# The first two row tiles of x in two transfers instead of one

## The chip, the cores and the metric

The kernel runs on one core of a Trainium2 chip. The metric is device time in microseconds (us): the median of three runs of the kernel before is 456.29 us (456.26 to 456.68).

## The reference

A graph network of three edge convolutions on N = 2500 nodes with 256 features and 80000 edges, sorted by target. Cut to what matters:

```python
h = maximum(layernorm(x), 0)                        # by row of x
xs = [h]
for W, b in ((W0, b0), (W1, b1), (W2, b2)):
    m = concat([h[dst], h[src] - h[dst]]) @ W + b   # one row for each edge
    s = segment_sum(m, dst, N)
    h = relu(s / maximum(count_of_edges, 1)[:, None])
    xs.append(h)
out = x + concat(xs) @ Wf + bf
```

## The kernel before, in words

Since a sum over edges is linear, the kernel builds the matrix of counts A (how often node m is a source of node n) and computes each layer as a product of A with h @ W_bottom, plus h @ (W_top - W_bottom). The 2500 rows of x lie in 20 tiles of 128 rows (the last has 68); the tile `acc` holds x by row tile (`acc[:, t, :]`), and later the running output.

The beginning, about the first 32 us, does three things side by side, in an order written out by hand as a string of short names, one for each step; each engine takes its own instructions strictly in that order:

- It prepares the search for the edges: `dst_i`, the list of targets, is loaded (line 434, on ACT's queue). VectorE casts its first column into `first`, a product on TensorE shifts it, VectorE makes masks (`after`, `behind`, `pick`), and at the end `start_i` holds where each block of edges begins. GpSimd then gathers the edges (`ed`, `es`) with it. Two copies of the edge lists in DRAM, `src_e` and `dst_e`, lengthened at the end, serve the last gather.
- It normalizes x, two row tiles at a time: `stats` (lines 746 to 754) takes mean and variance on VectorE (`st`, `mv`), ACT and VectorE make scale and offset (`rs`, `off`), and VectorE, ACT or GpSimd normalizes the tile in place. TensorE transposes it into `hT` and multiplies it with the weights (`own_w`).
- It builds A window by window: VectorE compares node numbers (`one_m`, `one_n`), and TensorE multiplies these masks.

The string of steps begins (st0 is the statistic of tiles 0 and 1, st1 of 2 and 3, st2 of 4 and 5, st4 of 8 and 9, st7 of 14 and 15):

```
dstr lim first st0 sq0 next pi0 pk00 sc0 pk01 pi1 sg00 of0 Nm0 T0 st1 se00 sg01 pk10 st2 se02 R0 sq1 sc1
of1 sg10 se01 se03 pk21 sg21 Z0 Np1 pk31 sg31 st4 T1 st7 ...
```

Loads of x go through `load_x` (line 438) by the list `chunks` (line 443): tiles 0 and 1, and 2 to 5, on SP's queue, tiles 6 to 11 on ACT's queue, then on SP's queue, between the weights, tiles 12 to 15 and 16 to 19 (the last, of 68 rows, by a transfer of its own). A transfer counts up one of eight completion semaphores, which the tile framework hands out in turn; a transfer that reuses one waits, on the issuing engine, until the one before it on that semaphore has landed, and what stands behind it on the engine waits too.

After the beginning, TensorE runs through the three layers and the final product.

Of the kernel before, what the change touches and what calls it, by code (L numbers as in the profile page):

```python
# [298 lines left out]
def by_windows(ctx: ExitStack, tc: tile.TileContext, x, src, dst, Ws, bs, Wf, bf, out, missing):  # L299
    nc = tc.nc  # L300
    PE, DVE, ACT, POOL, SP = nc.tensor, nc.vector, nc.scalar, nc.gpsimd, nc.sync
    PEo, DVEo, POOLo, ACTo, SPo = (InOrder(tc, e) for e in (PE, DVE, POOL, ACT, SP))
# [3 lines left out]
    NT = (N + P - 1) // P  # L306
# [131 lines left out]
    def load_x(queue, a, b):  # L438
        queue.dma_start(acc[:, a:min(b, NT - 1), :], xr[:, a:min(b, NT - 1), :])
        if b == NT:  # L440
            queue.dma_start(acc[:LAST, NT - 1, :], x[(NT - 1) * P:N, :])

    chunks = [(0, 2), (2, 6), (6, 12), (12, 16), (16, NT)]
    load_x(SPo, *chunks[0])
    load_x(SPo, *chunks[1])
    load_x(ACTo, *chunks[2])
    ws = [None] * L
    wfs = [None] * (L + 1)
    raws = [None] * (L + 1)
# [6 lines left out]
    def load_wb(l, queue=SP):  # L456
        if l:
            new_raw(l)
        ws[l] = wpool.tile([P, DC, D], F32, name="wt"), raws[l][:, :, 0, :] if l else hot.tile([P, DC, D], F32, name="own_w0", bufs=1)
        queue.dma_start(ws[l][1], Ws[l][D:2 * D, :].rearrange("(c p) d -> p c d", p=P))  # L460

    def load_wt(l, queue=SP):
        queue.dma_start(ws[l][0], Ws[l][0:D, :].rearrange("(c p) d -> p c d", p=P))

    def load_wf(l, queue=SP):
        if l == L:
            new_raw(l)
        wfs[l] = raws[l][:, :, 1, :] if l else hot.tile([P, DC, D], F32, name="own_w1", bufs=1)
        queue.dma_start(wfs[l], Wf[l * D:(l + 1) * D, :].rearrange("(c p) d -> p c d", p=P))

    load_wb(0, SPo)
    load_x(SPo, *chunks[3])
    load_wf(0, SPo)
    load_x(SPo, *chunks[4])
    load_wt(0, SPo)

    line_i = pp.tile([P, 1], I32, name="line_i")
# [1111 lines left out]
def gnn_kernel(tc: tile.TileContext, x, src, dst, Ws, bs, Wf, bf, out):  # L1589
    nc = tc.nc  # L1590
    with tc.tile_pool(name="flag", bufs=1) as flag:
        missing = flag.tile([1, 1], I32, name="missing")
        tc.mark_branch_hint_location("again", "LikelyTaken",
                                     engines=[getattr(mybir.EngineType, e) for e in ("PE", "DVE", "Activation")])
        near_end = by_windows(tc, x, src, dst, Ws, bs, Wf, bf, out, missing)
        loads, (again,) = nc.values_load_multi_w_load_instructions(missing, min_val=0, max_val=1)

        for d in loads:
            if d.ins.engine in [getattr(mybir.EngineType, e) for e in ("PE", "DVE", "Activation")]:
                tc.add_manual_dep(d.ins, near_end.ins.name,  # L1600
                                  mybir.DependencyInfo(mybir.DependencyClass.Sync, mybir.DependencyReason.DATA),
                                  reason="behind the outputs")
        with tc.If(again > 0, label="again"):
            general(tc, x, src, dst, Ws, bs, Wf, bf, out)
# [28 lines left out]
```

## Time and profile before

| | |
|---|---|
| median of three runs | 456.29 us |
| the profiled execution's own time | 456.32 us |
| its span, from first to last instruction | 454.4 us |
| mean granted TensorE clock | 0.998 |
| TensorE busy | 447.2 us, 98% of the span |
| VectorE busy | 379.3 us, 83% |
| ScalarE (ACT) busy | 327.7 us, 72% |
| GpSimd (POOL) busy | 52.0 us, 11% |

Busy shares are averages over the whole span; the change lies in its first 12 us, so the tables by stage and the timeline of that stretch say more. All times of the trace are counted from the span's start. Nearly every instruction carries line 267, a helper that records it in program order, so groups are told apart by the names of their tiles. A line of the timeline gives start, length, engine, line, instruction, output<-input, shapes, and in brackets how long the engine had been idle before it and what ended that. For an issue of a transfer (SPq, ACTq) the length is that of the issue on its engine, not that of the data.

### The profile page before, as it was taken

What the parts mean: (1) busy time and instruction counts of PE and PEld (TensorE: products, weight loads), DVE (VectorE), ACT (ScalarE), POOL (GpSimd) and SP (SyncE); (2) the same over time, 40 slices, a digit from 0 to 9 for tenths busy, and PEclk for the clock granted to TensorE, in tenths of its full rate; (3) what the DMA queues carried; (4) which work ended last, traced back from release to release, by engine and by line L of the source; (5) the groups of instructions that cost most, each with busy time, mean ns of one, the idle gap of its engine ahead of it and who ended that gap; (6) DMA issues with size and microseconds to landing.
All of it is one profiled execution on the core that took longest, in us unless ns stands there. A gap on an engine that the chain in (4) does not pass through costs nothing.

```text
span 454.4 us, 7514 instructions
## 1 busy us (share of the span) xinstructions
PE 447.2 (98%) x2749; PEld 360.6 (79%) x2749; DVE 379.3 (83%) x736; ACT 327.7 (72%) x608; POOL 52.0 (11%) x68
## 2 busy tenths in 40 slices
PE   8999999999999999999999999999999999999996
PEld 4878877888888888878877878877888778788795
DVE  7999999998899645399958968996999589598996
ACT  5898888777764445587879968875877899597730
POOL 4781201302015010100000000000000000000000
PEclk9999999999999999999999999999999999999999
DMA  8410198792949995611393442211114924322015
GB/s 277 117 36 1 33 202 154 86 160 45 207 93 122 189 244 123 145 47 45 103 359 124 137 169 93 91 45 47 46 53 135 337 92 147 127 92 91 1 52 178
DMA packets 28776, 55.05 MB, mean 121 GB/s; under 512 B 1995, under 2 KB 20126, under 8 KB 28734
## 3 DMA queue, kind: packets, MB, share of 16 engines
q0 software_dynamic: 12576, 19.06, 25.4%
q1 hardware_dynamic: 14654, 33.83, 22.2%
q10 hardware_dynamic: 1504, 1.63, 1.1%
q8 instruction: 22, 0.36, 0.3%
q14 instruction: 20, 0.16, 0.1%
HBM read 36.47 MB, written 18.20 MB: 120 GB/s over the span
## 4 chain that ended last, share of the span: by engine, by line
PE 92%; POOL 2%; DMA 2%; DVE 2%; issue 1%; ACTq 0%; POOLq 0%
PE bank L267 92%; DMA acc<-in_x_dram 2%; POOL acc L267 1%; DVE st L267 1%; POOL es L267 1%; POOL ed L267 0%; DVE acc L267 0%; DVE mv L267 0%; ACTq L267 0%; DVE end_f L267 0%; DVE start_i L267 0%; DVE rs L267 0%; DVE ends L267 0%; DVE off L267 0%; DVE lead L267 0%
## 5 line engine op out<-in xcount | busy, mean ns | idle before, releaser
L267 ACT CAST block<-staged 128x1008 fp32r<-128x1008 bf16 x120 | 117.6, 1029 | 3.5 <-ACT block L267 3.1
L267 PE MATMUL bank<-a,zh 128*128 128x504 f32 (+1 forms) x200 | 80.3, 401 | 0.0
L267 PE MATMUL bank<-block,zh 128*128 128x504 f32 (+1 forms) x200 | 79.0, 395 | 0.0
L267 PE MATMUL bank<-a,zl 128*128 128x504 f32 (+1 forms) x200 | 77.9, 389 | 0.0
L267 PE MATMUL bank<-block,zl 128*128 128x504 f32 (+1 forms) x200 | 77.2, 386 | 0.0
L267 ACT CAST a<-bank 128x480 fp32r<-128x480 f32 (+1 forms) x105 | 53.2, 570 | 26.5 <-PE bank L267 26.4
L267 DVE TENSOR_TENSOR one_m<-iota_m,key_m 128x2048 bf16<-128x2048 bf16 (+2 forms) x55 | 64.3, 1168 | 6.2 <-PE bank L267 5.8
L267 PE MATMUL bank<-block,sh 128*128 128x504 f32 x160 | 69.1, 432 | 0.0
L267 PE MATMUL bank<-block,sl 128*128 128x504 f32 x160 | 62.5, 391 | 0.0
L267 PE MATMUL bank<-block,staged 128*128 128x512 f32 (+1 forms) x288 | 62.4, 368 | 0.0
L267 PEld LDWEIGHTS bank<-block,staged 128*128 128x128 f32 x288 | 49.4, 188 | 9.9 <-issue 0.4
L267 DVE TENSOR_TENSOR block<-staged 128x1008 fp32r<-128x1008 bf16 x40 | 46.7, 1204 | 4.2 <-PE bank L267 3.4
L267 PEld LDWEIGHTS bank<-block,zh 128*128 128x128 f32 x200 | 37.6, 188 | 8.6 <-issue 0.4
L267 PEld LDWEIGHTS bank<-block,zl 128*128 128x128 f32 x200 | 37.5, 188 | 8.2 <-issue 0.4
L267 PEld LDWEIGHTS bank<-a,zl 128*128 128x128 f32 x200 | 37.7, 188 | 7.4 <-issue 0.5
L267 PEld LDWEIGHTS bank<-a,zh 128*128 128x128 f32 x200 | 37.6, 188 | 7.4 <-issue 0.5
L267 DVE TENSOR_TENSOR one_n<-iota_n,key_n 128x640 bf16<-128x640 bf16 (+2 forms) x110 | 42.5, 428 | 0.0
L267 PEld LDWEIGHTS bank<-block,sh 128*128 128x128 f32 x160 | 30.1, 188 | 10.6 <-issue 2.8
L267 PEld LDWEIGHTS bank<-block,sl 128*128 128x128 f32 x160 | 30.1, 188 | 9.4 <-issue 3.7
L267 PEld LDWEIGHTS <-one_m 128*128 128x128 bf16 x834 | 29.2, 98 | 7.4 <-issue 3.7
L267 PE MATMUL bank<-own_w,hT 128*128 128x256 f32 x144 | 34.6, 384 | 0.0
L267 PE MATMUL bank<-one_n,one_m 128*128 128x60 bf16 x834 | 32.5, 195 | 0.0
(198 smaller groups left out, 667.3 us busy)
## 6 DMA issues: line engine op xcount, KB each, us to landing
staged<-a_dram SPq DMA_DIRECT2D x52, 504.0 KB
a_dram<-a POOLq DMA_DIRECT2D x24, 630.0 KB, 9.3
acc<-in_x_dram POOLq DMA_DIRECT2D x3, 640.0 KB, 20.7
out_dram<-acc SPq DMA_DIRECT2D x5, 256.0 KB
acc<-in_x_dram SPq DMA_DIRECT2D x2, 512.0 KB
acc<-in_x_dram ACTq DMA_DIRECT2D x1, 768.0 KB
out_dram<-acc SPq DMA_DIRECT2D x5, 128.0 KB
wt<-in_L_gnn_W_dram SPq DMA_DIRECT2D x2, 256.0 KB
```

The lines of the kernel that those rows point to most:

```text
L267: return self.tc.keep_in_program_order(call(*args, **kwargs))
```

## The change

The entry (0, 2) of `chunks` becomes (0, 1) and (1, 2), and SP issues both. The entries behind it keep their tiles, queues and order.

```diff
-    chunks = [(0, 2), (2, 6), (6, 12), (12, 16), (16, NT)]
+    chunks = [(0, 1), (1, 2), (2, 6), (6, 12), (12, 16), (16, NT)]
     load_x(SPo, *chunks[0])
     load_x(SPo, *chunks[1])
-    load_x(ACTo, *chunks[2])
+    load_x(SPo, *chunks[2])
+    load_x(ACTo, *chunks[3])
...
     load_wb(0, SPo)
-    load_x(SPo, *chunks[3])
+    load_x(SPo, *chunks[4])
     load_wf(0, SPo)
-    load_x(SPo, *chunks[4])
+    load_x(SPo, *chunks[5])
     load_wt(0, SPo)
```

The first instructions on SP's queue, before the change. DMAHW0 to DMAHW7 are the eight semaphores; 128x2x256 is two row tiles; `own_w` and `wt` are weights, `brow` the rows of the bias:

```order
L267 DMA acc<-in_x_dram 128x2x256
L267 DMA acc<-in_x_dram 128x4x256
L267 DMA own_w_131<-in_L_gnn_W_dram 128x2x256
L267 DMA acc<-in_x_dram 128x4x256
L267 DMA own_w_134<-in_L_gnn_Wf_dram 128x2x256
L267 DMA acc<-in_x_dram 128x3x256
L267 DMA acc<-in_x_dram 68x256 [waits DMAHW0_49,DVE_49]
L267 DMA wt<-in_L_gnn_W_dram 128x2x256 [waits DMAHW1_49]
L505 DMA src_e<-in_src_dram 16x1250 [waits DMAHW2_49]
L495 DMA brow<-in_L_gnn_b_dram 1x256 [waits DMAHW3_49,Pool_49]
L495 DMA brow<-in_L_gnn_b_dram 1x256 [waits DMAHW4_49]
L504 DMA es_161<-in_src_dram 1x128 [waits DMAHW5_49,Pool_49]
```

The same place after the change:

```order
L267 DMA acc<-in_x_dram 128x256 x2
L267 DMA acc<-in_x_dram 128x4x256
L267 DMA own_w_132<-in_L_gnn_W_dram 128x2x256
L267 DMA acc<-in_x_dram 128x4x256
L267 DMA own_w_135<-in_L_gnn_Wf_dram 128x2x256
L267 DMA acc<-in_x_dram 128x3x256 [waits DMAHW0_49]
L267 DMA acc<-in_x_dram 68x256 [waits DMAHW1_49,DVE_49]
L267 DMA wt<-in_L_gnn_W_dram 128x2x256 [waits DMAHW2_49]
L506 DMA src_e<-in_src_dram 16x1250 [waits DMAHW3_49]
L496 DMA brow<-in_L_gnn_b_dram 1x256 [waits DMAHW4_49,Pool_49]
L496 DMA brow<-in_L_gnn_b_dram 1x256 [waits DMAHW5_49]
L505 DMA es_162<-in_src_dram 1x128 [waits DMAHW6_49,Pool_49]
```

There is one more issue at the head, so every issue behind it comes one place later, and the semaphores are handed out one further on. The wait for DMAHW0, which is that of `dst_i`, moves from the last 68 rows of x to the transfer of tiles 16 to 18. In the kernel before, `src_e` waits for DMAHW2, the transfer of tiles 2 to 5; now it waits for DMAHW3, and which transfer that is follows from VectorE's rows. Two places there: the first statistics (the BN_STATS rows, each of one row tile), behind the memset of `first`, and further on the statistic of tile 2. The first place, before:

```order
L267 MEMSET first 1x1 [waits DVE_49]
L267 BN_STATS st<-acc 128x6 [waits DMAHW1_49]
L267 BN_STATS st<-acc 128x6
L267 BN_AGGR mv<-st 128x2 [waits DVE_49] x2
L267 TENSOR_TENSOR after<-bank_228,after 128x1 [waits PE_49]
```

and after:

```order
L267 MEMSET first 1x1 [waits DVE_49]
L267 BN_STATS st<-acc 128x6 [waits DMAHW1_49]
L267 BN_STATS st<-acc 128x6 [waits DMAHW2_49]
L267 BN_AGGR mv<-st 128x2 [waits DVE_49] x2
L267 TENSOR_TENSOR after<-bank_229,after 128x1 [waits PE_49]
```

Tile 1's statistic now has a wait of its own; the order of VectorE's instructions is the same. The second place, up to the statistic of tile 2, after the change:

```order
L267 RECIPROCAL rs<-rs 128x2 [waits Activation_49]
L267 TENSOR_SCALAR behind<-limr_i,after 128x384
L267 SCALAR_TENSOR_TENSOR pick<-limr_i,first,behind 128x384 [waits DVE_49]
L267 SCALAR_TENSOR_TENSOR off<-mv,rs 128x2
L267 TENSOR_SCALAR acc<-acc,mv,rs 128x256
L267 BN_STATS st<-acc 128x6 [waits DMAHW4_49]
```

The last row waited for DMAHW2 before. So tiles 2 to 5 now have DMAHW4, and DMAHW3 stays with ACT's transfer of tiles 6 to 11: `src_e` now waits for that one, and the first `brow` row for tiles 2 to 5, the other way round than before.

## The prediction

> **What bounds the kernel now.** I read the page's first part, then the chain of waits, then busy time by stage, and last the instructions of SP, ACT and DVE in the first 12 us, where the change acts. The page and the table by stage (stretch in us, its length, then busy us and instructions of PE, PEld, DVE, ACT, POOL, the clock, the share of the 16 DMA engines, GB/s):
>
> ```profile
> span 454.4 us, 7514 instructions
> ...
> PE 447.2 (98%) x2749; PEld 360.6 (79%) x2749; DVE 379.3 (83%) x736; ACT 327.7 (72%) x608; POOL 52.0 (11%) x68
> ...
> 4.47:10.28 5.81, 5.37 (x22) 2.76 (x22) 5.56 (x28) 4.31 (x14) 0.73 (x2) 1.00 1.06 345
> 10.28:17.63 7.35, 7.35 (x42) 6.65 (x41) 7.33 (x37) 6.18 (x21) 5.56 (x6) 1.00 0.59 178
> ...
> 32.17:450.06 417.89, 417.87 (x2566) 338.50 (x2566) 350.76 (x619) 302.32 (x539) 30.15 (x31) 1.00 0.49 119
> ```
>
> From 32.17 us on TensorE is busy 417.87 of 417.89 us at full clock: nothing there waits for a load of x. What the change can move is the moment at which that stretch begins, one for one. Which work sets it stands in the chain of waits (start, length, what):
>
> ```profile
> 1.24 9.04 DMA acc<-in_x_dram
> ...
> 10.30 0.75 DVE st L267 x2
> ...
> 21.50 0.95 POOL es L267
> ...
> 32.17 417.89 PE bank L267 x2566
> ```
>
> The chain goes back to the transfer that ACT issued at 1.24 (row tiles 6 to 11) and through the row statistics on VectorE. VectorE is the narrow place of this stage: 5.56 of 5.81 us and then 7.33 of 7.35 us busy. A stall of it there, or an earlier start, goes through to the end with little lost. So the question is narrow: does VectorE start earlier or stall?
>
> **Where the loads and VectorE stand.** First the issues of SP and ACT, then VectorE with one weight load of TensorE (start, length, engine, instruction, what it waited for):
>
> ```profile
> 0.73 0.46 SPq L267 DMA_DIRECT2D acc<-in_x_dram  x1
> 0.81 0.40 ACTq L267 DMA_DIRECT2D dst_i<-in_dst_dram  x1
> 1.24 0.49 ACTq L267 DMA_DIRECT2D acc<-in_x_dram  x1
> 1.25 0.46 SPq L267 DMA_DIRECT2D acc<-in_x_dram  x1
> 1.75 0.51 SPq L267 DMA_DIRECT2D own_w<-in_L_gnn_W_dram  x1
> ...
> 3.49 0.47 SPq L267 DMA_DIRECT2D acc<-in_x_dram  x1
> ...
> 7.25 0.62 SPq L505 DMA_DIRECT2D src_e<-in_src_dram  x1
> 10.35 0.54 SPq L495 DMA_DIRECT2D brow<-in_L_gnn_b_dram  x2
> 11.09 0.22 SPq L504 DMA_DIRECT2D es<-in_src_dram  x1
> ```
>
> ```profile
> 4.47 0.15 DVE L267 CAST first<-dst_i 128x1 f32<-128x1 int32 x1 [1.86 <-DMA dst_i<-in_dst_dram]
> 4.67 0.42 DVE L267 BATCH_NORM_STATS2 st<-acc 128x6 f32<-128x256 f32 x1
> 4.68 0.06 DVE L267 MEMSET first<- 1x1 f32 x1
> 4.85 0.51 PEld L267 LDWEIGHTS bank<-first,shift 128*128 128x128 f32 x2 [0.97 <-POOL back_b L513]
> 5.00 0.41 DVE L267 BATCH_NORM_STATS2 st<-acc 128x6 f32<-128x256 f32 x1
> 5.55 0.12 DVE L267 TENSOR_TENSOR after<-bank,after 128x1 f32<-128x1 f32 x1
> ...
> 7.74 0.75 DVE L267 BATCH_NORM_STATS2 st<-acc 128x6 f32<-128x256 f32 x2
> ...
> 10.30 0.75 DVE L267 BATCH_NORM_STATS2 st<-acc 128x6 f32<-128x256 f32 x2
> 11.19 0.72 DVE L267 BATCH_NORM_STATS2 st<-acc 128x6 f32<-128x256 f32 x2
> ...
> 17.98 0.30 DVE L267 TENSOR_SCALAR lo_i<-es 128x256 int32<-128x256 int32 x1
> ```
>
> The first statistic of x at 4.67 stands behind two instructions on `dst_i`, which VectorE had awaited for 1.86 us: the cast at 4.47 that ends at 4.62, and a memset that needs the cast. So the 256 KB of tiles 0 and 1 were not what VectorE was held by for any time that shows: at most the 0.05 us from 4.62 to 4.67.
>
> **The change, part by part.** It takes out one issue of 256 KB and puts in two of 128 KB; the bytes and their order on SP's queue stay.
>
> 1. *Tile 0 comes earlier.* Its cover is `dst_i`. Even with tile 0 there at 3 us, the statistic cannot pass the cast and memset ahead of it. Gain: between 0 and 0.05 us (4.67 - 4.62), and the next step, 5.55, waits for a product on TensorE whose weight load began at 4.85 behind the memset, so not even that need come through. I take 0. If `dst_i` were not in the way, the cover would be gone and the gain would be tile 0's lead, which the next rows bound.
>
> 2. *`dst_i` itself could land earlier*, if tile 1's half leaves the DMA engines to it for a while. The packets of 0 to 2 us, then the rows of 3 to 4 us, and last of 4 to 4.5 us (q1 is SP's, q10 ACT's; packets, MB, share of the engines):
>
> ```profile
> DMA packets 18, 0.02 MB, mean 9 GB/s; under 512 B 0, under 2 KB 18, under 8 KB 18
> ...
> DMA packets 278, 0.38 MB, mean 382 GB/s; under 512 B 28, under 2 KB 193, under 8 KB 278
> q10 hardware_dynamic: 100, 0.21, 55.6%
> q1 hardware_dynamic: 178, 0.17, 49.9%
> ...
> q1 hardware_dynamic: 175, 0.18, 102.2%
> q10 hardware_dynamic: 1, 0.00, 0.1%
> ```
>
> Both queues share the engines while `dst_i` flows. At most tile 1's whole 128 KB would step aside: 131 KB / 382 GB/s = 0.34 us. But tile 1 is issued at about 0.73 + 0.52 = 1.25 us, where now the third tile is, well before tile 0's half can be through (the first row: 18 packets by 2 us), so the queue holds work all along. I take 0; bound 0.34 us of gain.
>
> 3. *One more issue on SP.* Price 0.46 us of the queue for 256 KB and 0.22 us for the smallest (es), 0.52 us from start to start at most. It pushes back, up to the load of `wt`, everything behind it: the 512 KB of tiles 2 to 5 from 1.25 to 1.75, the weights, tiles 12 to 15, and so on. Hidden by the queue's own backlog: in 4 to 4.5 us SP's queue alone fills the engines (102.2%) with what had been issued by 1.71. A transfer that is handed over 0.5 us later behind such a backlog lands no later. Bound if the backlog did not cover it: 0.52 us on a VectorE stall. The nearest place is the statistic at 7.74 of tiles 2 and 3; SP's wait below shows their transfer landed at about 7.25, so even there 0.5 us of slack stands against 0.52. The statistic at 11.19 reads tiles 12 and on; no row shows when those land, so there the bound stands in full. I take 0, the row being nearest to a queue that is never empty; bound 0.5.
>
> 4. *Waits that move.* Eight completion semaphores go round, and every issue waits for the one that used its semaphore before. SP's waits (total, times, longest):
>
> ```profile
> SPq L495 <- DMA acc<-in_x_dram: 2.4, 1, 2.4
> SPq L505 <- DMA acc<-in_x_dram: 1.3, 1, 1.3
> ```
>
> The instruction order shows the load of tiles 16 to 18 now behind `dst_i`, so it goes out at 4.47 and not 3.49: 1 us late. Its data are last in a backlog that keeps the engines over 100% (table: 1.06 up to 10.28), so the late hand-over is free. The copy of `src` into `src_e` changed its partner: it waited 1.3 us for tiles 2 to 5 and went out at 7.25; now it waits for ACT's 768 KB, which landed at 10.28. That is 3 us later, and behind it on SP stand the two `brow` rows (10.35 to about 11.0) and the `es` row (11.09 to about 11.6). `src_e` is read by the gather at 21.50 (the chain's POOL es), `es` by VectorE at 17.98: slack of 6 us and more. Cost 0; the bound without that slack would be 0.5 us, the shift of `es`.
>
> Sum: 0 + 0 + 0 + 0 on a profiled execution of 456.32 us (span 454.4 and 1.9 us around it), which lies 0.03 us above the median of 456.29 us. **Forecast: no change, 456.3 us**, with the small terms between -0.39 us (0.05 + 0.34) and +0.5 us.
>
> A rule that speaks against the change: the Trainium skill, "DMA: Bandwidth & Descriptors", section "Rules for kernel authors", wants many small transfers coalesced into a large one, and its section on the anatomy of one DMA puts a fixed cost of about 2 us on each. The trace shows issues on SP 0.5 us apart with their data back to back, so that cost overlaps here. Were it paid in a row, the sum would be about +2 us; that is the last rival below.
>
> **The rivals.**
>
> *Earlier start.* Items 1 and 2 at their bounds together: 456.3 - 0.39 = 455.9 us. For it: VectorE is full and passes a gain on. Against it: `dst_i`, 312.5 KB in one piece on the other queue, still starts the stage. Even in full it is -0.09%.
>
> *A transfer of SP's is held behind ACT's 768 KB (slower).* ACT issued tiles 6 to 11 at 1.24, yet in 4 to 4.5 us its queue moved one packet while SP's (2 to 5, issued at 1.25) moved 175. So an issued transfer can be held for 3 us while the other queue runs, and the two issues lie 0.01 us apart. Now tile 1 takes the place at 1.25, and tiles 2 to 5 come at 1.75, after ACT's. If the order of issue decides, 768 KB go ahead of 512 KB: from 4.0 us, 1.31 MB at about 352 GB/s take 3.7 us, to 7.7, and 0.5 us from last packet to use (as `dst_i`: last packets before 4.0, used at 4.47) make 8.2, against the statistic at 7.74: a stall of about 0.5 us, 456.8 us. If tile 1 itself falls behind the 768 KB: 0.786 / 0.352 = 2.2 us from 4.0, 0.4 us for its own 128 KB and 0.5 us give 7.1 against 5.00: a stall of 2.1 us, 458.4 us. It decides as soon as tiles 2 to 5 land after 7.74. Against it: the bytes moved by 10.28 are the same, and tile 1 has the very place that tiles 2 to 5 had. The skill bears on it from two sides: "Perfetto Trace Analysis", section on HWDGE instructions, has one shared descriptor generator that is locked until one transfer's descriptors are all made, by which such a hold is possible; "DMA: Bandwidth & Descriptors", "Issuing engines are not separate DMA queues", has the queues interleave, with which the single packet of q10 does not agree.
>
> *Each transfer pays a fixed cost in a row.* A further transfer ahead of all others would then cost VectorE about the whole time of one small load; the nearest row is the distance from issue to use of `dst_i`, 4.47 - 0.81 = 3.7 us, less what overlaps. I set half of it, +1.9 us, as an estimate: 458.2 us. Against it: SP's five issues up to 3.49 would take 18 us one after the other, and tiles 2 to 5 were there at 7.25.
>
> **How the numbers follow.** Forecast 0.81; earlier start 0.08; held behind the 768 KB 0.09 (0.05 for 456.8, 0.04 for 458.4); fixed cost in a row 0.02. A measurement of this kernel tells a change from none at about 0.2%, 0.9 us. Slower by that: 0.04 + 0.02, and 0.01 of the case of 456.8: 0.07. Faster: the bound of -0.39 us does not reach it, so only what I have not seen, 0.04. Same: 0.89. The range takes both bounds (455.9 and 456.8) and as much again as three runs differ (0.42 us) on either side: 455.5 to 457.2 us.
>
> **What would show it right or wrong.** Right: VectorE's cast of `dst_i` within 0.1 us of 4.47, the first statistic right behind it, no DMA named as releaser of a statistic, the two statistics at 7.74 and 10.30 within 0.3 us, and the TensorE stretch beginning at 32.2 +- 0.4. Step 4 shows as `src_e` issued near 10.3. Step 3 is wrong if VectorE waits for a load of x at 5.00, 7.74 or 11.19. The forecast fails if that stretch starts over 0.9 us off, or if its 417.9 us themselves change, for which I know no cause.

## The result, and the profile after

The changed kernel took 459.23 us (median; 458.92 to 460.30), the kernel before 456.49 us beside it (456.26 to 457.09). The ratio is 1.0054, 95% interval 1.0038 to 1.0069: 2.7 us slower, where no change was forecast.

The page of the kernel after: span, busy time by engine, and the row of q8, a queue that fetches instructions (packets, MB, share of 16 engines).

```profile
span 457.2 us, 7516 instructions
...
PE 447.2 (98%) x2749; PEld 360.4 (79%) x2749; DVE 379.5 (83%) x736; ACT 327.6 (72%) x608; POOL 52.6 (11%) x68
...
q8 instruction: 23, 0.38, 0.3%
```

Busy time is the same on every engine to within 0.6 us, and the span is 2.8 us longer (457.2 against 454.4). So the time went into waiting. There are two instructions more: the added issue on SP and one other. The chain of waits says where to look (start, length, what):

```profile
8.57 0.75 DVE st L267 x2
...
17.86 0.34 DVE st L267
...
18.31 0.11 POOL ed L267
...
28.46 3.81 POOL acc L267 x2
...
32.31 417.90 PE bank L267 x2566
...
450.23 0.48 DVE acc L267
```

TensorE's long stretch begins at 32.31 instead of 32.17 and lasts 417.90 instead of 417.89 us. The beginning, where the change acts, cost 0.14 us. The rest lies behind TensorE's last product. Busy time by stage of the kernel after, and below it the last stage of the kernel before (stretch, length, busy us and instructions of PE, PEld, DVE, ACT, POOL, clock, DMA share, GB/s):

```profile
32.31:450.21 417.90, 417.88 (x2566) 338.51 (x2566) 350.46 (x619) 302.19 (x539) 30.12 (x31) 1.00 0.49 119
450.21:457.20 6.99, 0.00 (x0) 0.00 (x0) 0.48 (x1) 0.00 (x0) 0.00 (x0) 0.75 0.26 83
```

```profile
450.06:454.40 4.34, 0.00 (x0) 0.00 (x0) 0.48 (x1) 0.00 (x0) 0.00 (x0) 0.84 0.40 130
```

The tail grew from 4.34 to 6.99 us: 2.65 us, with no engine busier in it. 0.14 + 0.01 + 2.65 = 2.80 us is the whole difference of the spans.

What the tail holds is the end of the program. At its end every engine reads a flag, and a branch jumps over a fallback for unusual inputs (`general`, under `tc.If(again > 0)`, line 1604 after, 1603 before), which these inputs do not take. A hint for TensorE, VectorE and ACT says that this jump is likely, so that its target can be fetched early; it is one of the first instructions of each program and runs at 0.7 to 0.8 us, 451 us ahead of the branch. The instructions of the branch's line (engine's sequencer, operation, count: ns, when), before:

```profile
L1603 PEldq COMPARE_BRANCH  x1: 398/398/398, 452.1 to 452.1; - x1
L1603 DVEq COMPARE_BRANCH  x1: 90/90/90, 452.1 to 452.1; - x1
L1603 SPq COMPARE_BRANCH  x1: 53/53/53, 450.3 to 450.3; - x1
L1603 PEldq EVENT_SEMAPHORE  x1: 51/51/51, 452.6 to 452.6; - x1
```

and after:

```profile
L1604 PEldq COMPARE_BRANCH  x1: 3702/3702/3702, 452.3 to 452.3; - x1
L1604 DVEq COMPARE_BRANCH  x1: 90/90/90, 452.3 to 452.3; - x1
L1604 PEldq EVENT_SEMAPHORE  x1: 51/51/51, 456.1 to 456.1; - x1
```

TensorE's branch starts 0.2 us later and takes 3702 ns instead of 398 ns; VectorE's takes 90 ns in both. TensorE's next instruction comes at 456.1 instead of 452.6. SP, which collects the ends of all engines, then waits for it. SP's semaphore instructions at the end of the program (count: shortest, median and longest ns, when), before and after:

```profile
L1627 SPq EVENT_SEMAPHORE  x14: 17/28/28, 452.8 to 454.4; - x14
```

```profile
L1628 SPq EVENT_SEMAPHORE  x14: 17/28/2462, 453.1 to 457.1; - x14
```

The longest of them, 2462 ns, is a wait for TensorE, which the kernel before does not have (total us, times, longest, after):

```profile
SPq L1628 <- PEq L1604: 2.5, 1, 2.5
```

Of the branch's 3.30 us more, 2.65 show in the span, because in the kernel before SP was busy with these instructions until 453.5 in any case, 0.9 us longer than TensorE needed to get there (452.6).

The queue q8 moved one packet in the last 5 us before, and two after (window 452.2 to 457.2, before and after):

```profile
q8 instruction: 1, 0.02, 1.2%
```

```profile
q8 instruction: 2, 0.03, 2.8%
```

Each packet is about 0.38 MB / 23 = 16.5 KB. The Trainium skill, "Runtime: NRT & Kernel Launch", section "Instruction fetch mechanics", states that engines refill their instruction memory in 16 KiB blocks of 256 instructions, and that a taken branch whose target is not there must wait for a fetch. The size of the packets agrees, and if the branch waited for such a fetch, the 3.3 us are its price here.

What has a change of two loads to do with TensorE's last branch? TensorE's instructions where it transposes tiles 0 and 1 of x, with their waits, before and after:

```
L267 MATMUL bank_256<-shift,acc 128x128 [waits DMAHW1_49,DVE_49]
L267 MATMUL bank_256<-shift,acc 128x128
L267 MATMUL bank_256<-shift,acc 128x128 [waits Activation_49]

L267 MATMUL bank_257<-shift,acc 128x128 [waits DMAHW1_49,DVE_49]
L267 MATMUL bank_257<-shift,acc 128x128
L267 MATMUL bank_257<-shift,acc 128x128 [waits DMAHW2_49,Activation_49]
```

Tile 1 now comes by a transfer of its own, so its first transpose waits for that transfer too. An instruction that waits for two semaphores gets an instruction of its own for one of them: TensorE executes 71 instructions that only wait, where it had 70. That is the second added instruction. Everything behind it on TensorE, the last branch included, stands one place further on in memory.

The beginning did not stay as it was either. VectorE, and the issues of SP and ACT, after:

```profile
4.43 0.15 DVE L267 CAST first<-dst_i 128x1 f32<-128x1 int32 x1 [1.37 <-DMA dst_i<-in_dst_dram]
4.63 0.42 DVE L267 BATCH_NORM_STATS2 st<-acc 128x6 f32<-128x256 f32 x1
4.97 0.41 DVE L267 BATCH_NORM_STATS2 st<-acc 128x6 f32<-128x256 f32 x1
...
8.57 0.75 DVE L267 BATCH_NORM_STATS2 st<-acc 128x6 f32<-128x256 f32 x2 [0.79 <-DMA acc<-in_x_dram]
```

```profile
0.73 1.35 SPq L267 DMA_DIRECT2D acc<-in_x_dram  x3
...
1.22 0.45 ACTq L267 DMA_DIRECT2D acc<-in_x_dram  x1
...
7.75 0.68 SPq L506 DMA_DIRECT2D src_e<-in_src_dram  x1
```

Tile 2's statistic waits 0.79 us for x; it started at 7.74 before and waited for nothing. `src_e`, which now waits for ACT's 768 KB, went out at 7.75, so those 768 KB had landed by then, where the kernel before used them at 10.30. ACT's transfer of tiles 6 to 11 has overtaken SP's of tiles 2 to 5. What the queues moved from 4.4 to 5.4 us, before and then after (q1 is SP's, q10 ACT's; packets, MB, share):

```profile
q1 hardware_dynamic: 211, 0.22, 67.4%
q10 hardware_dynamic: 83, 0.08, 32.2%
```

```profile
q10 hardware_dynamic: 371, 0.38, 107.8%
```

After the change SP's queue moves nothing for this microsecond. How 0.8 us of stall became 0.14 us is in the chain: VectorE's last statistic ends late enough to put GpSimd's gather (`ed`) at 18.31 instead of 17.63 (+0.68), but GpSimd's normalization at the end of the stage starts at 28.46 instead of 28.24 (+0.22): the kernel before had GpSimd idle there for 1.27 us, waiting for VectorE's `rs`.

```profile
28.24 5.08 POOL L267 TENSOR_SCALAR acc<-acc,mv,rs 128x256 f32<-128x256 f32 x3 [1.27 <-DVE rs L267]
```

### The profile page after: what moved, and what is told of

The parts are those of the page before. It is cut to its first block, busy times and chain, and to the rows that moved or that the text cites. A ratio compares the mean times of both kernels' runs of the same rounds, so it can differ in the third digit from the quotient of the medians.

```text
span 457.2 us, 7516 instructions
## 1 busy us (share of the span) xinstructions
PE 447.2 (98%) x2749; PEld 360.4 (79%) x2749; DVE 379.5 (83%) x736; ACT 327.6 (72%) x608; POOL 52.6 (11%) x68
## 4 chain that ended last, share of the span: by engine, by line
PE 91%; POOL 3%; DVE 2%; DMA 2%; issue 1%; SPq 0%; POOLq 0%
PE bank L267 91%; DMA acc<-in_x_dram 2%; POOL acc L267 1%; DVE st L267 1%; POOL es L267 1%; POOL ed L267 1%; DVE mv L267 0%; DVE acc L267 0%; SPq L267 0%; DVE end_f L267 0%; DVE start_i L267 0%; DVE off L267 0%; DVE rs L267 0%; DVE ends L267 0%; DVE lead L267 0%
```

## The experiments

Three things were to be settled: whether the lost time is really that of the branch; which of the two matters, the place of the branch or that of its target; and why tiles 2 to 5 came late.

### The change with two TensorE instructions fewer

TensorE has products on an idle tile ahead of some steps (`WARM`) whose results nothing reads. One fewer is two instructions fewer (weight load and product).

```diff
-    WARM = {"next": 7, "pk00": 3, "T0": 3, "Z0": 2}
+    WARM = {"next": 6, "pk00": 3, "T0": 3, "Z0": 2}
```

> The changed kernel with one of the seven warm-up products ahead of the first real product on TensorE left out: two instructions fewer in TensorE's program, transfers as changed. Theory A (the extra wait that the change gives TensorE makes its program one instruction longer, and that makes the branch at the end of the program miss its prefetched code): TensorE's branch falls from 3702 ns back to about 0.4 us, one instruction fetch fewer (22 on its fetch queue, not 23), and the time is about 456.6 us (before, plus 0.1 to 0.2 us for the later start of the TensorE stretch). Rival B (the late tiles 2 to 5, or the longer queue of SP, cost the time): nothing of that is touched, so 459.2 us, branch 3.7 us.

Measured: 457.04 us (456.47 to 457.72) against 457.10 (456.11 to 457.37), ratio 1.0006 [0.9997, 1.0016]. The loss is gone. The branch, and tile 2's statistic, which still waits:

```profile
L1604 PEldq COMPARE_BRANCH  x1: 393/393/393, 452.3 to 452.3; - x1
```

```profile
8.57 0.75 DVE L267 BATCH_NORM_STATS2 st<-acc 128x6 f32<-128x256 f32 x2 [0.91 <-DMA acc<-in_x_dram]
```

All that the change does to the loads is still there, and the time is that of before. So the loads cost nothing that this can measure (at most 0.16%, 0.7 us, by the interval), and the rest of the 2.7 us is the branch's.

### The kernel before with two TensorE instructions more

```diff
+        PEo.matmul(ahead[0][:, 0:1], idle[:, :P], idle[:, 0:1], start=True, stop=True)
```

> The kernel before, with one product of a single column more on TensorE, ahead of the first real one: two instructions more in TensorE's program, transfers as before. Theory A: the branch takes about 3.7 us in place of 0.4, 23 fetches, time about 459.0 us. Rival B: 456.4 us, branch 0.4 us.

Measured: 459.19 us (458.67 to 460.09), ratio 1.0048 [1.0030, 1.0066].

```profile
L1604 PEldq COMPARE_BRANCH  x1: 4002/4002/4002, 453.0 to 453.0; - x1
```

One product of a single column in the first 10 us, with no change to any load, makes the kernel before as slow as the change. The page of this run counts 22 fetches like the kernel before, where 23 were expected. But a page ends with the span, here at 458.2 us, and the second fetch begins just behind it. In a window of 452.5 to 459.5 us there are two, as after the change:

```profile
q8 instruction: 2, 0.03, 2.2%
```

### Which place matters: the branch's or its target's

The fallback lies between the branch and its target. One transpose more in it moves the target alone; one fewer in the changed kernel puts the target back before its old place and leaves the branch where the change put it. (In the second kernel the fallback, which does not run on these inputs, is incomplete.)

```diff
-            nc.tensor.transpose(row[:, j * P:(j + 1) * P], key[:, c:c + 1].to_broadcast([P, P]), ident)
+            for _ in range(2 if c == 0 else 1):
+                nc.tensor.transpose(row[:, j * P:(j + 1) * P], key[:, c:c + 1].to_broadcast([P, P]), ident)
```

> The kernel before, with one transpose more in the fallback that the branch jumps over: TensorE's program up to and with the branch is as before, but the code that the branch jumps to lies two instructions further. If the place of the target decides (theory A1): branch 3.7 us, about 459 us. If the place of the branch itself decides (theory A2): branch 0.4 us, 456.4 us. Rival B: 0.4 us, 456.4 us.

```diff
-            nc.tensor.transpose(row[:, j * P:(j + 1) * P], key[:, c:c + 1].to_broadcast([P, P]), ident)
+            if c != 5 * J:
+                nc.tensor.transpose(row[:, j * P:(j + 1) * P], key[:, c:c + 1].to_broadcast([P, P]), ident)
```

> The changed kernel, with one transpose left out of the fallback that is jumped over (that makes the fallback, which does not run here, incomplete): the branch stays where the change put it, the target lies one instruction ahead of its place in the kernel before. Theory A1 (target): branch 0.4 us, about 456.6 us. Theory A2 (branch): 3.7 us, 459.2 us. Rival B: 459.2 us.

Measured: 456.44 us and 458.77 us, one execution of each (before, beside them: 457.10). The branch, in the kernel before with the longer fallback, and in the changed one with the shorter:

```profile
L1604 PEldq COMPARE_BRANCH  x1: 393/393/393, 452.0 to 452.0; - x1
```

```profile
L1605 PEldq COMPARE_BRANCH  x1: 3562/3562/3562, 452.2 to 452.2; - x1
```

The branch's own place decides, and the target's does not.

### Without the hint

```diff
-                                     engines=[getattr(mybir.EngineType, e) for e in ("PE", "DVE", "Activation")])
+                                     engines=[getattr(mybir.EngineType, e) for e in ("DVE", "Activation")])
```

> The kernel before, without TensorE's prefetch hint for the branch at the end (VectorE's and ACT's stay); one instruction fewer on TensorE. If the change costs its time by a prefetch that fails (theory A), taking the hint away costs the same: branch about 3.7 us, time about 459 us. If the hint does nothing here, branch 0.4 us and 456.4 us.

Measured: 459.57 us in one execution, beside 456.75 us of the kernel before (456.24 to 458.08).

```profile
L1603 PEldq COMPARE_BRANCH  x1: 3538/3538/3538, 453.0 to 453.0; - x1
```

Without the hint TensorE's branch costs what it costs after the change, although it stands one instruction ahead of its old place, where the hint makes it short (393 ns in the first experiment). So the hint is what makes it short, and after the change it no longer helps.

### How far the slow places reach

The change with two instructions more (three more than before), and with 64 more (65 more than before: 37 single-column products, 74 instructions, less five products of `WARM`, 10).

```diff
+        PEo.matmul(ahead[0][:, 0:1], idle[:, :P], idle[:, 0:1], start=True, stop=True)
```

> The changed kernel with one single-column product more, so three instructions ahead of the branch more than in the kernel before (after the two slow places one and two). If the branch only has to stay out of the first instruction of a fetched block, it is fast again: 0.4 us. If all places past the edge are slow until the prefetch has time to run, still 3 to 4 us and about 459 us.

```diff
-    WARM = {"next": 7, "pk00": 3, "T0": 3, "Z0": 2}
+    WARM = {"next": 2, "pk00": 3, "T0": 3, "Z0": 2}
...
+        for _ in range(37):
+            PEo.matmul(ahead[0][:, 0:1], idle[:, :P], idle[:, 0:1], start=True, stop=True)
```

> The changed kernel with 64 instructions more on TensorE ahead of the branch (37 single-column products in place of five of the warm-up products). TensorE would now come into the block that holds the branch some 4 us or more before the branch; if the prefetch is asked for when that block is entered, it is done in time: branch 0.4 us, about 456.6 us. If not, 3.7 us and about 459 us, and the slow stretch is wider than 64 instructions.

Measured: 459.96 us and 457.22 us, one execution of each, beside 456.75.

```profile
L1605 PEldq COMPARE_BRANCH  x1: 4087/4087/4087, 452.8 to 452.8; - x1
```

```profile
L1606 PEldq COMPARE_BRANCH  x1: 398/398/398, 452.8 to 452.8; - x1
```

So the branch is short at -1 (the first experiment) and 0 instructions, long at +1, +2 and +3, short again at +65. An edge lies between 0 and +1, and some way behind it the branch is short once more.

When the packets of q8 come shows more. This queue follows TensorE's program: with the 64 more its first packet of the span comes at 17.6 instead of 21.4 us. In all kernels without the 64, short branch or long, the last packet ahead of the branch begins at 425.7 to 428.1 us, and then none until the branch. From the branch on, the eight kernels with a short branch have one packet, which begins after the branch is over; the five with a long branch have two. The second of these begins after the branch is over, like the one of the others; the first begins 0.9 to 1.5 us after the branch has begun, while it still runs. With 65 more there is a further packet ahead of the branch, at 444.3 us, 8.5 us before it (window 444 to 446), and one behind it:

```profile
q8 instruction: 1, 0.02, 2.7%
```

I read it so: the fetch that brings the target is asked for when TensorE's program goes over the edge of a block. Where the edge lies one to three instructions ahead of the branch, the branch has to wait for that fetch; with 65 it is long done. That fits all six places and the sizes of the packets. But the packets carry no addresses, so which code each brought was not seen, nor where exactly the edge lies.

### Why tiles 2 to 5 come late

In the rival of the prediction the order of issue decides: tiles 2 to 5 are now the last of SP's three issues of 0.73 to 2.08, from about 1.6 us, behind ACT's at 1.22, where before the two lay 0.01 us apart. First I moved ACT's issue behind its table load in the program:

```diff
-    load_x(ACTo, *chunks[3])
...
     ACTo.activation(warm, ones, AF.Sqrt)
+    load_x(ACTo, *chunks[3])
```

> The changed kernel with two instructions fewer on TensorE (so that the branch is fast), and ACT's 768 KB of tiles 6 to 11 issued about 2 us later, behind ACT's table load and first activation at about 3.2 us; the transfers of SP as in the change. If tiles 2 to 5 came late because ACT's 768 KB had been issued ahead of them (theory C), they now land near 7.2 us and the statistic of tile 2 starts at 7.7 without a wait (8.57 with 0.8 to 0.9 us of wait in the change), while tiles 6 to 11 land at 10.3 or later. If they were late because SP issued them half a microsecond later, the wait stays. Time 456.5 us if tiles 6 to 11 still land by 10.5, later by what they are late otherwise.

Measured: 457.57 us (456.78 to 457.73), ratio 1.0013 [1.0002, 1.0024]; tile 2's statistic at 8.56 with a wait of 0.94 us, as without the edit. By these numbers alone the order of issue would fall. ACT's own timeline shows otherwise:

```profile
1.22 1.28 ACT L267 ACT_TABLE_LOAD   x1 [1.22 <-PEq L1620]
1.29 0.39 ACTq L267 DMA_DIRECT2D acc<-in_x_dram  x1
2.52 0.20 ACT L267 ACTIVATE warm<-ones 128x1 f32<-128x1 f32 x1
```

The issue went out at 1.29, while the table load was still running: it stands behind the load in the program and does not wait for it. The edit moved the issue by 0.07 us (1.29 for 1.22), still ahead of SP's at about 1.6, and the run says nothing about the order of issue.

Another reading is that the place of a transfer in its own queue decides. Two runs put tiles 2 to 5 in second place on SP's queue with the split (tile 1 issued by ACT), and in third place without it (`own_w` ahead):

```diff
-    load_x(SPo, *chunks[1])
+    load_x(ACTo, *chunks[1])
     load_x(SPo, *chunks[2])
```

> The change with two TensorE instructions fewer, and tile 1 issued by ACT between dst_i and the 768 KB, so that tiles 2 to 5 are SP's second transfer again and the 768 KB are ACT's third. Theory D (a transfer runs by its place in its own queue: the queues take turns by transfers, so tiles 2 to 5, third on SP's queue after the change, came behind ACT's second): tiles 2 to 5 land early again, the statistic of tile 2 starts at 7.7 without waiting for a transfer, src_e goes out at about 7.3 or later than 10, and the 768 KB land only at about 10.3. Theory E (the split itself, one more small transfer in the beginning, delays tiles 2 to 5 wherever it is issued): the statistic of tile 2 still starts at about 8.5 with a wait of 0.8 to 0.9 us. Time under either: 456.5 to 457.5, the same as before, with TensorE's final branch at about 0.4 us.

```diff
-    load_x(SPo, *chunks[1])
-    load_x(ACTo, *chunks[2])
...
     load_wb(0, SPo)
+    load_x(SPo, *chunks[1])
+    load_x(ACTo, *chunks[2])
```

> The kernel before with tiles 0 and 1 in one transfer, and the weights own_w (256 KB) moved ahead of tiles 2 to 5 on SP's queue, so that tiles 2 to 5 are SP's third transfer without any split of x. Theory D (place in the own queue decides): tiles 2 to 5 run behind ACT's 768 KB, the statistic of tile 2 starts at 8.5 to 9 after a wait of 0.7 us or more, and the 768 KB land by about 8. Theory E (the split is what delays): tiles 2 to 5 still run ahead of the 768 KB and are late only by the 256 KB of the weights ahead of them, 262 KB / 352 GB/s = 0.7 us: they land at about 7.9 instead of 7.25, a wait of about 0.3 us, and the 768 KB land after 10 us. Time: 456.3 to 457.5 under either, if TensorE's final branch takes 0.4 us.

Measured: 457.96 us (456.05 to 459.14) against 457.00 (456.09 to 457.64), ratio 1.0025 [1.0009, 1.0041], so somewhat above the 456.5 to 457.5 us expected, for which no run here gives the cause; and 457.8 us in one execution. VectorE, tile 1 on ACT's queue, then the weights ahead:

```profile
5.33 0.43 DVE L267 BATCH_NORM_STATS2 st<-acc 128x6 f32<-128x256 f32 x1 [0.65 <-DMA acc<-in_x_dram]
...
8.09 0.75 DVE L267 BATCH_NORM_STATS2 st<-acc 128x6 f32<-128x256 f32 x2
...
10.87 0.75 DVE L267 BATCH_NORM_STATS2 st<-acc 128x6 f32<-128x256 f32 x2 [0.28 <-DMA acc<-in_x_dram]
```

```profile
9.53 0.75 DVE L267 BATCH_NORM_STATS2 st<-acc 128x6 f32<-128x256 f32 x2 [1.54 <-DMA acc<-in_x_dram]
```

That the split itself delays is out: with it, tile 2 comes without a wait in the one kernel, and without it, it comes 1.8 us late in the other (at 9.53, later than the 8.5 to 9 expected). But both runs fit the order of issue as well as the place in the queue, since an earlier place is also an earlier issue. The last run keeps the place and changes the time alone. ACT writes one column of tile 6 ahead of the transfer, so that the transfer must wait for ACT's work:

```diff
+    DVE.memset(ones, 1.0)
+    ACTo.activation(acc[:, 6, 0:1], ones, AF.Sqrt)
     load_x(ACTo, *chunks[3])
...
-    DVE.memset(ones, 1.0)
```

> The change with two TensorE instructions fewer, and ACT's 768 KB really issued late: ACT first writes one column of tile 6, behind its table load, and the transfer over that tile waits for it, so its issue moves from 1.2 to about 2.7 us, behind the issue of tiles 2 to 5 (about 1.6 us) and that of own_w (2.1 us). Place in the queue is unchanged: tiles 2 to 5 third on SP's queue, the 768 KB second on ACT's. Theory C (order of issue decides which of two waiting transfers runs first): tiles 2 to 5 go ahead, the statistic of tile 2 starts at about 7.7 or before without a wait for a transfer, and the 768 KB land at 10 us or later. Theory D (place in the own queue decides): the 768 KB still go ahead, the statistic of tile 2 starts at 8.5 us or later after a wait of 0.8 us or more, and SP's queue moves next to nothing while ACT's runs. Time under either 456.3 to 457.6, with TensorE's final branch at about 0.4 us.

Measured: 458.67 us beside 457.32, one execution of each, above the 456.3 to 457.6 us expected. The issue, and VectorE:

```profile
2.75 0.41 ACTq L267 DMA_DIRECT2D acc<-in_x_dram  x1
```

```profile
7.71 0.74 DVE L267 BATCH_NORM_STATS2 st<-acc 128x6 f32<-128x256 f32 x2
8.62 0.74 DVE L267 BATCH_NORM_STATS2 st<-acc 128x6 f32<-128x256 f32 x2
12.79 0.76 DVE L267 BATCH_NORM_STATS2 st<-acc 128x6 f32<-128x256 f32 x2 [1.75 <-DMA acc<-in_x_dram]
```

and the two queues from 4.4 to 5.4 us:

```profile
q1 hardware_dynamic: 358, 0.36, 106.9%
```

Now SP's queue has the engines to itself, tile 2 is there at 7.71, and the 768 KB come late, 1.75 us after VectorE could have used them. Tiles 2 to 5 are still third on SP's queue, so the place in the queue falls and the order of issue stands. It held for the weights too: by 6 us ACT's queue has moved nothing of the 768 KB, and SP's has moved 0.95 MB, more than the 0.79 MB of tiles 0 to 5; so most of the weights that SP had issued at 2.12, ahead of ACT's 2.75, went first as well. Here the price is no longer absorbed: TensorE's stretch begins at 34.19. None of these kernels is faster than the one before by more than its times scatter.

## Why the prediction was wrong

*The sum.* The step that failed is the frame of the sum: "the span 454.4 and 1.9 us around it", in which only the beginning of TensorE's stretch could move. I named the 417.9 us as what else could change, and they did not (417.90). What lies between TensorE's last product and the end, 4.34 us, I took as fixed and did not read. It grew by 2.65 us of the 2.80. The instruction order showed the added wait on VectorE, and I did not look at TensorE's, which also has one. Nor did I count a wait as an instruction that moves all behind it. With that counted, the price could still not have been read off the trace of before, which has no slow branch; but a branch of 398 ns under a hint, with SP waiting for the end of every engine, was there to be named as a rival with an unknown price. The forecast's own signs did not cover the step: neither of the two that were to make it fail came (the stretch over 0.9 us off, its 417.9 us changed), and it failed all the same.

*Item 1, tile 0 earlier, 0.* Right: the first statistic starts at 4.63 instead of 4.67, behind `dst_i`, which stays the cover.

*Item 2, `dst_i` earlier, 0.* Right: its cast starts at 4.43 instead of 4.47.

*Item 3, one more issue on SP, 0, since "a transfer that is handed over 0.5 us later behind such a backlog lands no later".* Wrong. Tiles 2 to 5 were handed over about 0.4 us later (about 1.6 for 1.25) and used at 8.57 instead of 7.74, after a wait of 0.79 us: more than the 0.5 us that I had as the bound. The backlog is not one queue but two, and a later issue let the other queue's 768 KB go first. The stall was then not passed on "with little lost": 0.79 became 0.68 at the gather and 0.14 at TensorE, because GpSimd had 1.27 us of waiting further on that took it up. So two errors of this item nearly cancel: that the 0 came out within 0.14 us at TensorE is luck, and the sign set for it, the statistic at 7.74 within 0.3 us and no transfer named as its releaser, failed. The starts of the stretch scatter by more than that between profiles whose loads are those of before (32.17, 32.04 with the longer fallback, 33.02 without the hint), so even the 0.14 us is not clear of them.

*Item 4, the waits that move, 0.* Right in cost, wrong in time: `src_e` went out at 7.75, not near 10.3, as ACT's 768 KB were early.

*The rivals.* The hold behind ACT's 768 KB did happen, in its first form and by the order of issue, as the last run shows. Its stall was 0.79 us against the 0.5 us worked out. The term that was mis-sized is the 0.5 us from last packet to use: SP's queue had moved the 0.79 MB of tiles 0 to 5 by 7.7 us, as worked out, and the statistic began 0.87 us later. The price of the stall was in the end 0.14 us against 0.5. Tile 1 itself did not fall behind (its statistic starts at 4.97). The rival lay on the slower side, but its time of 456.8 us does not explain 459.2. The earlier start came with 0.04 us at the cast and was lost in the stall. A fixed cost in a row is out: without the slow branch the split costs 0.06% [-0.03, 0.16], not the 0.4% of 458.2 us.

## What to carry to other kernels

An edit counts all the instructions that it puts into an engine's program, the waits included, and a branch at the end can be worth more than the edit itself: when a change of the loads moves the time by a few microseconds and no busy time, compare the tail behind the last product first. Two or three instructions put in or taken out elsewhere on the same engine tell such an effect of place from an effect of the edit, for the price of one run. And where two queues feed one stage, the order of issue between them is part of the schedule: 0.4 us decided here which of two transfers ran first.

## What the runs showed of the hardware

- A branch on TensorE that jumps over the fallback took 393 to 398 ns in eight of these kernels and 3.5 to 4.1 us in five, by its own place in the program, or for want of its hint; the same branch on VectorE takes 90 ns, on SP 53 ns.
- The prefetch hint is no guarantee: one instruction more ahead of the branch took its effect away, 64 further ones gave it back. A long branch goes with one more 16 KB instruction packet, begun 0.9 to 1.5 us into the branch, in all five kernels that have it, and in none of the eight others.
- Of two transfers issued 0.4 us apart or more on two queues, the earlier issued one ran first, and for a microsecond nearly alone (371 packets to 0, or 358 to 0, by the order of issue). Issued 0.01 us apart, SP's ran alone at first (175 packets to 1 from 4 to 4.5 us), and then they shared the engines (138 to 140 from 5 to 6 us).
- ACT issued a transfer at 1.29 us while its table load ran from 1.22 to 2.50: an issue behind a table load is not held by it.
